# The gate beside the shared expert's weights, a token a partition, and a filter product of three multiplications

## The chip, the cores and the metric

The kernel runs on one core of one Trainium2 chip. The metric is the device time of one execution in microseconds; the time before is the median of three runs. The engines are called PE (TensorE; PEld is its weight load), DVE (VectorE), ACT (ScalarE), POOL (GpSimd) and SP (SyncE, which here only issues transfers).

## The reference

A layer of two halves, in float32, over x of 8 sequences x 512 tokens x 256 channels, each half with a residual and a layer norm after it.

```python
# first half: a gated long convolution
u = x @ W_in + b_in                        # 256 -> 768
x0, x1, v = split(short_conv3(u))          # three taps a channel
v = v * x1
k = (sin(sin(pe @ W1 ...) @ W2 ...) @ W3 + b3) * exp(-t * deltas)   # the filter, 512 x 256
v = irfft(rfft(pad(v), 1024) * conj(rfft(k, 1024)))[:512] + filter_bias
x = layernorm(x + (v * x0) @ W_out + b_out)

# second half: 16 experts, 4 a token, and a shared expert
probs = softmax(x @ gate_w.T)              # 16 logits a token
top_w, top_idx = top_k(probs, 4); top_w = top_w / sum(top_w)
moe = sum over the token's 4 experts of top_w * (silu(x @ w1.T) * (x @ w3.T)) @ w2.T   # hidden 128
shared = (silu(x @ sw1.T) * (x @ sw3.T)) @ sw2.T
x = layernorm(x + moe + shared)
```

The reference computes all experts for every token and weighs them; the kernel sorts the tokens' rows by expert and computes only the chosen four.

## The kernel before

**An order that is planned ahead.** Nothing is scheduled by the framework: `manual_schedule` keeps every engine's instructions in the order in which they are emitted. That order comes from `Plan`, a list scheduler that runs while the kernel is built. Each piece of work is a generator that yields `turn(engine, cost, needs, rings, table, rank)` and then emits its instructions; `Plan.run` keeps a clock for each engine, takes the turn that can start first, breaks ties within 0.05 us by rank, and adds 1.3 us where an activation table must change. Costs are microseconds written by hand into each turn. Buffers are part of it: `ps` are the 8 banks of PSUM, `b2` six buffers of 2 KB a partition, `b4` nine of 4 KB, and a turn waits until one is free. A change of one cost or one need can therefore move everything that comes after it.

**The first half, for each sequence b.** `front` multiplies the input in 128x512 tiles (L418), `convolve_short` evicts each twice (L401, L402) and adds two shifted taps on DVE (L407). The gated v is transposed (L461), and `half_transform` multiplies even and odd tokens with cosines and sines (L484); `joined` adds and subtracts them into `vf`, of real and imaginary part, two halves m of 128 frequencies. `product` multiplies `vf` with the filter's transform. Its first two steps make three operations of 1024 columns for each part (L515 to L517); steps three and four make four operations of 512 columns each (L527 to L530) and complete the second half, c=1. There `g0` holds the filter's first part and `hf` its second part with a sign. `convolved_full` is the way back: for each half i of the channels and each c it takes four matmuls of 256 columns (L560), in the order part 0, part 1 of c=0, then of c=1. `FULL` is 8, so for all eight sequences `product` returns before its last lines, and `convolved` with `inv_sb` is never used. `gated_y`, `normed` and `scaled` finish the half (L598, L666, L625, L642).

**Routing and the shared expert.** `turned` transposes the normed rows x1 into `x1t`, channels on the partitions (L699), and spawns `router` and `shared`. `router` multiplies with the gate: x1t is the stationary side, and 16 columns move (L711), eight matmuls a sequence. DVE copies the logits beside eight columns of -3e38 (L723, L724), takes the top eight, marks the top four (`match_replace`, L741), and ACT takes the exponentials (L735). `shared` multiplies the other way round: sw1 or sw3 is stationary, and 512 tokens move (L797), four matmuls, so that the hidden units are on the partitions as the next product wants them. Then come silu on ACT (L803), one multiply on DVE (L808), sw2 (L818), and the addition to x1 (L842). `route` counts rows and writes each token's four places into `at` (L874); `scatter` sends x1's rows there with 16 indirect transfers on POOL (L996), each 128 rows.

**The experts.** Tokens are taken in four batches: sequences 0 and 1, 2 and 3, 4 and 5, then 6 and 7, the first three with one sort. When a batch's rows are counted, `listed` makes its list of tiles of 128 rows; `fetch` loads four tiles at a time, and `expert_pair` does two: transposes (L1181), w1 and w3 (L1195), silu and multiply (L1206, L1209), a transpose (L1215), w2 (L1227), the weight of the token on ACT or DVE, whichever clock is behind in the plan (L1238, L1240), and indirect transfers home on POOL (L1249). POOL's queue holds the scatters and these transfers in one order. At the end `returned` and `add_up` fetch each token's four results and `finished` norms them.

**The filter.** `filter_transform` runs once, first, and ends with four operations that fill `hf` (L1080) and a copy that fills `g0_sb` (L1088); every product needs them.

The constant and weight loads stand in SP's queue in the order of the code; `w_sb` holds all experts' weights, 17 x 256 columns by three.

Of the kernel before, what the change touches and what calls it, by code (L numbers as in the profile page):

```python
# [20 lines left out]
P = 128  # L21
# [3 lines left out]
NX = NE + 1  # L25
# [3 lines left out]
FULL = 8  # L29
# [174 lines left out]
def layer(  # L204
# [21 lines left out]
    inv: bass.AP,  # L226
# [92 lines left out]
    inv_sb = const.tile([P, 2, CH], F32, name="inv_sb")  # L319
    load(inv_sb, inv.rearrange("(k p) t -> p k t", p=P), "inv")  # L320
# [6 lines left out]
    gate_sb = const.tile([P, KD, NE], F32, name="gate_sb")  # L327
    load(gate_sb, gate, "gate")

    w_sb = const.tile([P, 3, NX * D], F32, name="w_sb")  # L330
    load(w_sb[:, :, NE * D :], experts[NE], "w_shared")
# [171 lines left out]
    def product(b, vf, hf_):  # L503

        needs = [("vf", b, i, m) for i in range(2) for m in range(2)]
        for step in range(4):
            part = step % 2

            op = ALU.add if part else ALU.subtract
            if step < 2:  # L510
                yield turn("DVE", 3 * 1.22, [*needs, "hf"], ["pf"] if step == 0 else ())
                if step == 0:
                    pf, hp = sb("pf", 1, [P, 2, 2, 2, D], f"pf_{b}")
                fa = ring.tile([P, 2, 2, D], F32, tag="fa", name=f"fa_{b}_{part}")
                nc.vector.tensor_mul(fa, vf[:, 1], g0[1 - part])  # L515
                nc.vector.tensor_mul(pf[:, part], vf[:, 0], g0[part])
                nc.vector.tensor_tensor(pf[:, part], pf[:, part], fa, op)  # L517
                if step == 1:
                    plan.done(("vf2", b), late=0.0)
                    if b < FULL:  # L520
                        plan.done(("pf", b, 0))
                        plan.spawn(convolved_full(b, pf, hp), 2 + b * 0.01)
            else:
                yield turn("DVE", 2.1 + 0.69, [("vf2", b)])
                t2 = ring.tile([P, 2, 2, D], F32, tag="fa", name=f"ta_{b}_{part}")
                ta, tb = t2[:, 0], t2[:, 1]
                nc.vector.tensor_tensor(ta, vf[:, 0, :, 0, :], hf[:, part], ALU.mult)  # L527
                nc.vector.tensor_tensor(tb, vf[:, 1, :, 0, :], hf[:, 1 - part], ALU.mult)
                nc.vector.tensor_tensor(ta, ta, tb, op)
                nc.vector.tensor_add(pf[:, part, :, 1, :], pf[:, part, :, 1, :], ta)  # L530
        plan.let(hf_)
        if b < FULL:
            plan.done(("pf", b, 1))
            return

        yield turn("DVE", 2 * 1.22, (), ["b4:pe"])
        pe, he = sb("b4:pe", 0, [P, 2, 2, D], f"pe_{b}")
        nc.vector.tensor_tensor(pe, pf[:, :, 0], pf[:, :, 1], ALU.add)
        plan.done(("pf", b, 0))
        nc.vector.tensor_tensor(pf[:, :, 0], pf[:, :, 0], pf[:, :, 1], ALU.subtract)  # L540
        plan.done(("pf", b, 1))
        plan.spawn(convolved(b, (pe, pf[:, :, 0]), (he, hp)), 2 + b * 0.01)
# [7 lines left out]
    def convolved_full(b, pf, hp):  # L550
        for i in range(KD):
            for c in range(2):
                rings = [*(["ps"] if c == 0 else []), *(["b4:y"] if i == c == 0 else [])]
                yield turn("PE", 8 * PASS[CH], [("pf", b, c), "inv4"], rings)
                if i == c == 0:
                    y, hy = sb("b4:y", 0, [P, KD, T], f"y_{b}")
                if c == 0:
                    y_ps, h = ps([P, T], f"y_ps_{b}_{i}")
                for k in range(4):
                    nc.tensor.matmul(  # L560
                        y_ps[:, c * CH : (c + 1) * CH],
                        lhsT=pf[:, k // 2, k % 2, c, i * P : (i + 1) * P],
                        rhs=inv4_sb[:, k, :],
                        start=k == 0,
                        stop=k == 3,
                    )
            plan.done(("y_ps", b, i))
            plan.spawn(gated_y(b, i, y, y_ps, h), 2 + b * 0.01)
        plan.let(hp)
        plan.spawn(normed(b, y, hy), 2 + b * 0.01)  # L570

    def convolved(b, sums, held):
        for i in range(KD):
            for k in range(2):
                rings = [*(["ps"] if k == 0 else []), *(["b4:y"] if i == k == 0 else [])]
                yield turn("PE", 8 * PASS[P], [("pf", b, k), "inv"], rings)
                if i == k == 0:
                    y, hy = sb("b4:y", 0, [P, KD, T], f"y_{b}")
                if k == 0:
                    y_ps, h = ps([P, T], f"y_ps_{b}_{i}")  # L580
                for c in range(2):
                    for part in range(2):
                        nc.tensor.matmul(
                            y_ps[:, c * CH + k : (c + 1) * CH : 2],
                            lhsT=sums[k][:, part, c, i * P : (i + 1) * P],
                            rhs=inv_sb[:, part, k * P : (k + 1) * P],
                            start=part == 0,
                            stop=part == 1,
                        )
            plan.done(("y_ps", b, i))  # L590
            plan.spawn(gated_y(b, i, y, y_ps, h), 2 + b * 0.01)
        plan.let(*held)
        plan.spawn(normed(b, y, hy), 2 + b * 0.01)
# [97 lines left out]
    def turned(b):  # L691
        x1 = tiles["x1", b][0]
        for k in range(KD):
            yield turn("PE", 4 * PASS[P], [("x1", b)], ["ps", "b4:x1t"] if k == 0 else ["ps"])
            if k == 0:
                x1t, ht = sb("b4:x1t", 0, [P, KD, T], f"x1t_{b}", uses=2)
# [5 lines left out]
        plan.spawn(router(b, x1t, ht), 1)  # L702
        plan.spawn(shared(b, x1t, ht), 1.5)

    def router(b, x1t, ht):

        yield turn("PE", 1.7, [("x1t", b, 0), ("x1t", b, 1), "gate"], ["ps"])
        l_ps, h = ps([P, QT, NE], f"l_ps_{b}")
        for q in range(QT):
            for k in range(KD):  # L710
                nc.tensor.matmul(  # L711
                    l_ps[:, q, :],
                    lhsT=x1t[:, k, q * P : (q + 1) * P],
                    rhs=gate_sb[:, k, :],
                    start=k == 0,
                    stop=k == KD - 1,
                )
        plan.let(ht)
        plan.done(("l", b))
        plan.known["x1t", b] = plan.end  # L720
        yield turn("DVE", 1.3, [("l", b)], ["mask"])
        lg = ring.tile([P, QT, NE + 8], F32, tag="lg", bufs=2, name=f"lg_{b}")
        nc.vector.memset(lg[:, :, NE:], -BIG)  # L723
        nc.vector.tensor_copy(lg[:, :, :NE], l_ps)  # L724
        plan.let(h)
        top = ring.tile([P, QT, 8], F32, tag="top", bufs=2, name=f"top_{b}")
# [55 lines left out]
    def shared(b, x1t, ht):  # L782

        x1, h1 = tiles["x1", b]
        for s in range(2):
            yield turn(
                "PE",
                4 * PASS[T],
                [("x1t", b, 0), ("x1t", b, 1), "w_shared"],
                ["ps", "b2"] if s == 0 else ["ps"],  # L790
            )
            if s == 0:
                act, ha = sb("b2", 0, [P, T], f"acts_{b}")
            h_ps, h = ps([P, T], f"hs_ps_{b}_{s}")
            for k in range(KD):
                at = NE * D + s * HE
                nc.tensor.matmul(  # L797
                    h_ps, lhsT=w_sb[:, k, at : at + HE], rhs=x1t[:, k, :], start=k == 0, stop=k == KD - 1
                )
            plan.done(("hs", b, s))  # L800
            if s == 0:
                yield turn("ACT", 0.61, [("hs", b, 0)], table="silu")
                nc.scalar.activation(act, h_ps, AF.Silu)  # L803
                plan.let(h)
                plan.done(("acts", b))
        plan.let(ht)
        yield turn("DVE", 0.7, [("hs", b, 1), ("acts", b)])
        nc.vector.tensor_mul(act, act, h_ps)  # L808
        plan.let(h)
        plan.done(("actm", b))  # L810
        for q2 in range(QT // 2):
            yield turn("PE", 4 * PASS[D], [("actm", b)], ["ps", "b4:acc"] if q2 == 0 else ["ps"])
# [3 lines left out]
            for j in range(2):  # L816
# [3 lines left out]
                    lhsT=act[:, q * P : (q + 1) * P],  # L820
                    rhs=w_sb[:, 2, NE * D :],
# [208 lines left out]
    def filter_transform():  # L1030
# [45 lines left out]
        yield turn("DVE", 3.2, [("vf", "g", i, m) for i in range(2) for m in range(2)])  # L1076

        for m in range(2):
            for part in range(2):
                nc.vector.scalar_tensor_tensor(  # L1080
                    hf[:, part, m, :],
# [6 lines left out]
        nc.vector.tensor_copy(g0_sb, gf[:, :, :, 0, :])  # L1088
# [4 lines left out]
    hf = const.tile([P, 2, 2, D], F32, name="hf")  # L1093
    g0_sb = const.tile([P, 2, 2, D], F32, name="g0_sb")
    g0 = [g0_sb[:, part, :, None, :].to_broadcast([P, 2, 2, D]) for part in range(2)]
# [253 lines left out]
def shape_constants():  # L1349
# [28 lines left out]
    found = {"places": places, "tri": tri, "seg": np.concatenate(seg), "pos": pos, "decay": decay, "fwd": fwd, "inv": fwd.T / CH, "inv4": inv4, "sign": np.stack([even, -even], 1)}  # L1378
# [40 lines left out]
```

## Time and profile before

| | |
|---|---|
| three runs | 636.99, 639.95 and 643.25 us, median 639.95 |
| the profiled execution | 639.06 us, its span 637.2 us, mean granted clock of PE 0.949 |
| busy in the span | PE 564.1, PEld 423.8, DVE 471.7, ACT 351.9, POOL 320.1 us |
| moved by DMA | 114.33 MB, mean 179 GB/s |
| the chain that ended last | PE 38%, DVE 10%, DMA 4%, ACT 3% of the span, as far as it is followed back |

Busy time is the union of an engine's instructions, so their durations can add up to more. PE's matmuls are pipelined: the mean of one in a group is longer than the distance between two, and the chain, which counts the distance, is the place for prices. Each matmul is two records, a transpose is one. Lines such as L560 are those of the kernel before.

### The profile page before, as it was taken

To read this page: it belongs to the slowest core of one execution; us is meant where nothing else is said; L and a number is where in the kernel's file an instruction comes from. 1 tells how busy PE (TensorE), PEld (TensorE's weight loads), DVE (VectorE), ACT (ScalarE), POOL (GpSimd) and SP (SyncE) were. 2 spreads that over 40 slices of the span, in tenths; PEclk is the share of its full clock that TensorE was granted. 3 is DMA by queue.
4 is the path that set the end of the run, shared out by engine and by line. 5 is a ranking of instruction groups with operands and counts; after the bars stand their busy time and mean duration, and the time that the engine had idled before them with its cause. 6 is when DMAs were issued, how large, how long until landed. Compare 5 with 4: busy or idle time off the path is not lost.

```text
span 637.2 us, 9907 instructions
## 1 busy us (share of the span) xinstructions
PE 564.1 (89%) x2508; PEld 423.8 (67%) x2508; DVE 471.7 (74%) x1267; ACT 351.9 (55%) x737; POOL 320.1 (50%) x580
## 2 busy tenths in 40 slices
PE   5978989849999989899999999999989999889900
PEld 2436566427787756477976866898868888778700
DVE  3997898997986898598479668846633334888786
ACT  2432738404838527653845385275334556899855
POOL 0000018580028887048658841874887876447730
PEclk9997999969999999999999998999989999999955
DMA  7995006223306333335447561532876547999965
GB/s 263 353 333 166 17 34 201 75 102 126 108 29 202 115 133 135 108 111 180 158 150 243 177 214 61 181 132 79 271 227 194 167 140 220 302 356 323 347 230 213
DMA packets 67829, 114.33 MB, mean 179 GB/s; under 512 B 11435, under 2 KB 48569, under 8 KB 67774
## 3 DMA queue, kind: packets, MB, share of 16 engines
q1 hardware_dynamic: 54046, 78.02, 38.6%
q0 software_dynamic: 13728, 35.69, 15.3%
q8 instruction: 22, 0.36, 0.3%
q14 instruction: 33, 0.27, 0.1%
HBM read 61.51 MB, written 56.07 MB: 185 GB/s over the span
## 4 chain that ended last, share of the span: by engine, by line
PE 38%; DVE 10%; DMA 4%; ACT 3%; issue 2%; SPq 1%; POOL 1%; ACTq 0%; DVEq 0%; POOLq 0%
PE h_ps L1195 14%; PE o_ps L1227 7%; PE xr_ps L1181 3%; DMA xr<-xs 3%; PE hs_ps L797 2%; PE y_ps L560 2%; PE u_ps L418 2%; PE h_ps L1215 2%; PE z_ps L666 2%; DVE got L1297 2%; PE v_ps L484 1%; SPq L1127 1%; PE l_ps L711 1%; PE os_ps L818 1%; POOL results L1249 1%
## 5 line engine op out<-in xcount | busy, mean ns | idle before, releaser
L996 POOL DMA_INDIRECT xs<-x,at x128 | 133.7, 1044 | 189.0 <-DVE y L598 92.0
L1249 POOL DMA_INDIRECT results<-o,to x158 | 163.5, 1035 | 102.0 <-ACT o L1238 39.4
L1195 PE MATMUL h_ps<-w_sb,xrt 128*128 x632 | 149.6, 383 | 1.4 <-ACT xrt L1186 1.4
L1195 PEld LDWEIGHTS h_ps<-w_sb,xrt 128*128 128x128 f32 x632 | 118.4, 192 | 18.6 <-ACT xrt L1186 2.6
L418 PE MATMUL u_ps<-xt,w_in_sb 128*128 128x512 f32 x192 | 89.6, 605 | 4.1 <-DMA xt<-in_x_t 4.1
L1227 PE MATMUL o_ps<-w_sb,actt 128*128 x316 | 80.4, 383 | 5.6 <-ACT actt L1220 4.7
L560 PE MATMUL y_ps<-inv_sb,pf 128*128 128x256 f32 x256 | 68.9, 423 | 17.7 <-DVE pf L517 9.4
L401 ACT ACTIVATE u<-u_ps,chan_sb 128x512 f32<-128x512 f32 x48 | 32.9, 686 | 86.0 <-PE u_ps L418 28.2
L560 PEld LDWEIGHTS y_ps<-inv_sb,pf 128*128 128x128 f32 x256 | 51.9, 211 | 32.1 <-DVE pf L530 9.5
L1206 ACT ACTIVATE act<-h_ps 128x256 f32<-128x256 f32 (+1 forms) x80 | 29.9, 380 | 78.0 <-PE h_ps L1195 61.1
L1227 PEld LDWEIGHTS o_ps<-w_sb,actt 128*128 128x128 f32 x316 | 57.7, 190 | 18.3 <-ACT actt L1220 6.0
L418 PEld LDWEIGHTS u_ps<-xt,w_in_sb 128*128 128x128 f32 x192 | 35.8, 194 | 40.0 <-issue 38.2
L1209 DVE TENSOR_TENSOR act<-act,h_ps 128x256 f32<-128x256 f32 (+1 forms) x80 | 32.0, 412 | 34.7 <-ACT act L1206 34.5
L1186 ACT COPY xrt<-xr_ps 128x512 f32<-128x512 f32 (+1 forms) x80 | 44.9, 593 | 9.5 <-PE xr_ps L1181 8.5
L1238 ACT ACTIVATE o<-o_ps,sel 128x256 f32<-128x256 f32 x84 | 34.8, 473 | 23.3 <-PE o_ps L1227 20.5
L1181 PE MATMUL xr_ps<-ident,xr 128*128 128x128 f32 x316 | 45.3, 275 | 1.6 <-ACT xrt L1186 0.7
L1240 DVE TENSOR_TENSOR o<-o_ps,sel 128x512 f32<-128x512 f32 x37 | 25.4, 690 | 26.3 <-PE o_ps L1227 23.2
L1181 PEld LDWEIGHTS xr_ps<-ident,xr 128*128 128x128 f32 x316 | 37.1, 141 | 8.2 <-issue 3.1
L1220 ACT COPY actt<-h_ps 128x256 f32<-128x256 f32 (+1 forms) x80 | 28.7, 375 | 16.0 <-PE h_ps L1215 13.7
L1215 PE MATMUL h_ps<-ident,act 128*128 128x128 f32 x158 | 29.2, 276 | 4.9 <-DVE act L1209 4.9
L797 PE MATMUL hs_ps<-x1t,w_sb 128*128 128x512 f32 x64 | 33.4, 651 | 0.0
L666 PEld LDWEIGHTS z_ps<-w_out_sb,y 128*128 128x128 f32 x128 | 31.0, 327 | 2.3 <-issue 1.2
(164 smaller groups left out, 917.5 us busy)
## 6 DMA issues: line engine op xcount, KB each, us to landing
xr<-xs SPq DMA_DIRECT2D x158, 144.0 KB, 2.8
got<-results SPq DMA_DIRECT2D x32, 512.0 KB, 7.1
xs<-blank SPq DMA_DIRECT2D x62, 144.0 KB, 3.2
w_sb<-in_experts SPq DMA_DIRECT2D x17, 384.0 KB, 7.8
xt<-in_x_t SPq DMA_DIRECT2D x8, 512.0 KB
xn<-in_x SPq DMA_DIRECT2D x8, 512.0 KB, 4.5
kept<-acc SPq DMA_DIRECT2D x6, 512.0 KB, 3.7
sum<-kept SPq DMA_DIRECT2D x6, 512.0 KB, 4.6
```

Of the source, the lines that this page charges most:

```text
L418: nc.tensor.matmul(u_ps, lhsT=w_in_sb[:, k, m * P : (m + 1) * P], rhs=xt[:, k, :], start=k == 0, stop=k == KD - 1)
L560: nc.tensor.matmul(y_ps[:, c * CH : (c + 1) * CH], lhsT=pf[:, k // 2, k % 2, c, i * P : (i + 1) * P], rhs=inv4_sb[:, k, :], start=k == 0, ...
L666: nc.tensor.matmul(z_ps[:, j, :], lhsT=y[:, i, q::QT], rhs=w_out_sb[:, i, :], start=i == 0, stop=i == KD - 1,)
L797: nc.tensor.matmul(h_ps, lhsT=w_sb[:, k, at : at + HE], rhs=x1t[:, k, :], start=k == 0, stop=k == KD - 1)
L996: move = nc.gpsimd.indirect_dma_start(out=xs[i], out_offset=bass.IndirectOffsetOnAxis(ap=at[:, q, k : k + 1], axis=0), in_=x1[:, q, :], in ...
L1181: nc.tensor.transpose(t_ps[:, j, k, :], xr[:, j, k * P : (k + 1) * P], ident)
L1186: nc.scalar.copy(xrt[:, :n], t_ps[:, :n])
L1195: nc.tensor.matmul(h_ps[:, j, :], lhsT=xrt[:, j, k, :], rhs=w_sb[:, k, bass.ds(at[j], D)], start=k == 0, stop=k == KD - 1,)
L1215: nc.tensor.transpose(a_ps[:, j, :], act[:, j, :], ident)
L1227: nc.tensor.matmul(o_ps[:, j, :], lhsT=actt[:, j, :], rhs=w_sb[:, 2, bass.ds(at[j], D)], start=True, stop=True)
L1238: nc.scalar.activation(o[:, j], o_ps[:, j], AF.Copy, scale=sel[:, j0 + j, 0:1])
L1249: move = nc.gpsimd.indirect_dma_start(out=results[i], out_offset=bass.IndirectOffsetOnAxis(ap=to[:, j0 + j : j0 + j + 1], axis=0), in_=o[: ...
```

## The change

Two things are edited, and what was unused is removed.

The gate's 16 columns are loaded behind the shared expert's 256 in `w_sb`. A new `heads` multiplies, for each quarter q of a sequence, x1t as the stationary side with all 272 columns: logits, w1 and w3 come out in one bank of PSUM, a token a partition. `head` copies the logits on ACT, takes silu of 128 columns on ACT and multiplies on DVE, once for each q. The margin of -3e38 is written by POOL when `heads` begins. Since a token is now on a partition, `shared` transposes the four pieces, copies them on ACT, and goes on with sw2 as before.

`product` multiplies complex numbers with three multiplications: of re + im, of im and of re, by the filter's re, re + im and im - re, which are made once in `filter_transform`. Three operations of 1024 columns and twelve of 512 take the place of six and eight, and `vf` is written over. Its costs are new in both turns.

```diff
+    load(w_sb[:, :KD, NX * D :], gate)
+    load(w_sb[:, :, NE * D : NX * D], experts[NE], "w_shared")
...
     def product(b, vf, hf_):
...
+        yield turn("DVE", 4 * 1.22 + 2 * 0.69, [*needs, "hf"], ["pf"])
+        nc.vector.tensor_tensor(fa, re, im, ALU.add)
+        nc.vector.tensor_tensor(pf[:, 0], im, both(g0[:, 1]), ALU.mult)
+        nc.vector.tensor_tensor(pf[:, 1], re, both(g0[:, 2]), ALU.mult)
+        k = im[:, :, 1, :]
+        nc.vector.tensor_tensor(k, fa[:, :, 0, :], g0[:, 0], ALU.mult)
+        nc.vector.tensor_tensor(pf[:, 0, :, 0, :], k, pf[:, 0, :, 0, :], ALU.subtract)
+        nc.vector.tensor_tensor(pf[:, 1, :, 0, :], k, pf[:, 1, :, 0, :], ALU.add)
+        plan.done(("pf", b, 0))
+        plan.spawn(convolved_full(b, pf, hp), 2 + b * 0.01)
+        yield turn("DVE", 9 * 0.69)
+        second = fa[:, :, 1, :]
+        nc.vector.tensor_tensor(second, second, g0[:, 0], ALU.mult)
+        for part, by, of in ((0, 1, im), (1, 2, re)):
+            at = of[:, :, 0, :]
+            nc.vector.tensor_tensor(at, at, hf[:, by], ALU.mult)
+            nc.vector.tensor_tensor(pf[:, part, :, 1, :], pf[:, part, :, 1, :], at, ALU.add)
+        at = fa[:, :, 0, :]
+        nc.vector.tensor_tensor(at, at, hf[:, 0], ALU.mult)
+        nc.vector.tensor_tensor(second, second, at, ALU.add)
+        nc.vector.tensor_tensor(pf[:, 0, :, 1, :], second, pf[:, 0, :, 1, :], ALU.subtract)
+        nc.vector.tensor_tensor(pf[:, 1, :, 1, :], second, pf[:, 1, :, 1, :], ALU.add)
...
+    def heads(b, x1t, ht):
+        lg = ring.tile([P, QT, NE + 8], F32, tag="lg", bufs=2, name=f"lg_{b}")
+        nc.gpsimd.memset(lg[:, :, NE:], -BIG)
         for q in range(QT):
+            yield turn("PE", 1.0, [("x1t", b, 0), ("x1t", b, 1), "w_shared"], ["ps", "b2"] if q == 0 else ["ps"])
+            h_ps, h = ps([P, D + NE], f"hs_ps_{b}_{q}")
             for k in range(KD):
                 nc.tensor.matmul(
+                    h_ps,
                     lhsT=x1t[:, k, q * P : (q + 1) * P],
+                    rhs=w_sb[:, k, NE * D :],
...
+    def head(b, q, lg, act, h_ps, h):
+        yield turn("ACT", 0.25, [("hs", b, q)])
+        nc.scalar.copy(lg[:, q, :NE], h_ps[:, D:])
+        plan.done(("l", b, q))
+        yield turn("ACT", 0.35, (), table="silu", rank=1.5)
+        nc.scalar.activation(act[:, q, :], h_ps[:, :HE], AF.Silu)
+        plan.done(("silus", b, q))
+        yield turn("DVE", 0.25, [("silus", b, q)], rank=1.5)
+        nc.vector.tensor_mul(act[:, q, :], act[:, q, :], h_ps[:, HE:D])
...
     def router(b, lg):
-        nc.vector.memset(lg[:, :, NE:], -BIG)
-        nc.vector.tensor_copy(lg[:, :, :NE], l_ps)
...
     def shared(b, act, ha):
-                    h_ps, lhsT=w_sb[:, k, at : at + HE], rhs=x1t[:, k, :], start=k == 0, stop=k == KD - 1
-                nc.scalar.activation(act, h_ps, AF.Silu)
-        nc.vector.tensor_mul(act, act, h_ps)
+        yield turn("PE", 4 * PASS[P], [("actm", b, q) for q in range(QT)], ["ps"])
+        for q in range(QT):
+            nc.tensor.transpose(a_ps[:, q, :], act[:, q, :], ident)
+        yield turn("ACT", 0.6, [("as_ps", b)])
+        nc.scalar.copy(act, a_ps)
...
+        first = [gf[:, part, :, 0, :] for part in range(2)]
+        nc.vector.tensor_copy(g0[:, 0], first[0])
+        nc.vector.tensor_tensor(g0[:, 1], first[0], first[1], ALU.add)
+        nc.vector.tensor_tensor(g0[:, 2], first[1], first[0], ALU.subtract)
...
+        nc.vector.tensor_tensor(hf[:, 1], hf[:, 0], hf[:, 2], ALU.add)
+        nc.vector.tensor_tensor(hf[:, 2], hf[:, 2], hf[:, 0], ALU.subtract)
```

The four operations that fill `hf` stay, into places 0 and 2. `FULL`, `convolved`, `inv_sb` and `gate_sb` go.

## The prediction

> **What bounds the kernel now.** I read the page's parts 1 and 2 first, then the busy time by stage, then what TensorE (PE) waits for, then the chain for the price of one instruction of each kind, and last the groups by shape.
>
> ```profile
> PE 564.1 (89%) x2508; PEld 423.8 (67%) x2508; DVE 471.7 (74%) x1267; ACT 351.9 (55%) x737; POOL 320.1 (50%) x580
> PE   5978989849999989899999999999989999889900
> DVE  3997898997986898598479668846633334888786
> PEclk9997999969999999999999998999989999999955
> ```
>
> Two engines carry the span, one after the other. By stage (us, then busy us of PE, PEld, DVE, ACT, POOL):
>
> ```profile
> 16.00:300.00 284.00, 260.44 (x1005) 175.41 (x1004) 246.56 (x591) 142.37 (x263) 111.88 (x193) 0.95 0.42 139
> 300.00:447.00 147.00, 144.71 (x694) 115.42 (x693) 103.57 (x312) 83.95 (x180) 89.95 (x163) 0.99 0.48 158
> 447.00:603.00 156.00, 147.71 (x789) 127.76 (x787) 90.35 (x263) 100.59 (x232) 110.00 (x205) 0.99 0.77 253
> ```
>
> Up to 300 us PE and VectorE (DVE) are both nearly full (260 and 247 of 284) and take turns as the limit. From 300 to 603 us PE alone is: 292 of 303. After it 34 us of results coming home and a layer norm, which the change does not touch. What PE waits for in the first 300 us:
>
> ```profile
> PE y_ps L560 <- DVE pf L517: 9.4, 3, 5.4
> PE y_ps L560 <- DVE pf L530: 5.5, 6, 1.6
> ```
>
> So the filter's product on DVE, one of the two edited places, is what PE waits for; the other, the gate with the shared expert, is PE work itself. While PE waits, its clock falls (column after POOL):
>
> ```profile
> 45.00:48.00 3.00, 1.65 (x4) 0.86 (x4) 2.90 (x5) 0.00 (x0) 0.00 (x0) 0.80 0.76 249
> 48.00:51.00 3.00, 1.92 (x5) 1.18 (x4) 2.90 (x5) 0.00 (x0) 0.00 (x0) 0.50 0.92 300
> ```
>
> **PE's part.** The chain prices back-to-back passes (start, us, what):
>
> ```profile
> 317.67 1.69 PE l_ps L711 x16
> 354.58 3.45 PE h_ps L1195 x16
> 390.54 1.72 PE hs_ps L797 x4
> 429.13 0.87 PE x1t_ps L699 x8
> ```
>
> A matmul is two passes in the records, a transpose one. Taken out per sequence: the gate, 16 passes, 1.69 us (0.106 each though only 16 columns move); w1 and w3, 8 passes of 512 columns, 2 x 1.72 = 3.44. Put in: 16 passes of 272 columns. No row has 272; the 256-column row gives 3.45 for 16, the 512-column row 6.88, and 272 is nearest 256: both rows make 0.84 ns a column, so 0.23 each, 3.67 in all (3.45 and 6.88 kept as ends; the upper would lose 2.2 us a sequence). And four transposes back, 4 x 0.109 = 0.44. Net 1.69 + 3.44 - 3.67 - 0.44 = 1.02 us, times 8 = **8.2 us less PE work**. Pricing each program's whole list of PE instructions this way gives 530.1 us before and 521.7 after.
>
> **DVE's part.** Groups by shape (busy, mean ns):
>
> ```profile
> L1209 DVE TENSOR_TENSOR act<-act,h_ps 128x128 f32<-128x128 f32 x2 | 0.6, 283 | 0.6 <-ACT act L1206 0.6
> L515 DVE TENSOR_TENSOR fa<-vf,g_sb 128x1024 f32<-128x1024 f32 x16 | 19.6, 1222 | 0.2
> L527 DVE TENSOR_TENSOR ta<-vf,hf 128x512 f32<-128x512 f32 x16 | 11.0, 688 | 0.3
> L808 DVE TENSOR_TENSOR acts<-acts,hs_ps 128x512 f32<-128x512 f32 x8 | 5.5, 683 | 0.0
> L1206 ACT ACTIVATE act<-h_ps 128x128 f32<-128x128 f32 x2 | 0.6, 302 | 0.0
> L803 ACT ACTIVATE acts<-hs_ps 128x512 f32<-128x512 f32 x8 | 4.8, 597 | 3.3 <-PE hs_ps L797 2.3 <-ACT actt L1220 1.0
> ```
>
> Product before: 6 of 1024 and 8 of 512 columns, 6 x 1.22 + 8 x 0.69 = 12.84 us. After: 3 and 12, 3.66 + 8.28 = 11.94. That is 0.90 less a sequence, 7.2 in all. Its shape changes too. The first half that PE wants (c=0, part 0) was ready after three long operations, 3.66 us; now after three long and two short, 5.04. The last was ready at 12.84, now at 11.94. A PE that stands at the product therefore starts 1.4 us later and ends 0.9 us earlier. The shared multiply becomes four of 128: 4 x 0.283 - 0.683 = +0.45; the copy and the memset of the logits leave DVE (0.214 + 0.085): +0.15 net, 1.2 over 8. The set-up of the filter gains one copy of 512 for one of 1024 (0.69 by L1088, so 0.35 by half) and four operations of 0.69: +2.4, once, ahead of the first product where DVE is full. Sum: -7.2 + 1.2 + 2.4 = -3.6. The planner also moves two more expert outputs from DVE to ACT (35 instead of 37, 0.69 each): about **-5 us on DVE**.
>
> **ScalarE's (ACT) part.** Four copies of 128x16 (no such row; between 0.19 for the accumulator reads of one column at L625 and 0.256 for 128x64 at L735; I take 0.22), four silu of 128 for one of 512 (4 x 0.302 - 0.597 = +0.61), one copy of 512 (0.60, the x1t row of L436): +2.1 us a sequence, 17 in all, and four more L1238 instructions (the two outputs that DVE gives up, 0.473 each), 1.9 once. ACT is busy 55%, and its list holds 47 table loads before and after, so I cost this at nothing in throughput. Its cover is PE's expert tiles between a sequence's heads and its transposes; in sequences 0 to 2 only the four-matmul-pair z (3.4 us) stands there, and ACT needs 4 x (0.22 + 0.30) + 1.28 for the table = 3.4 us for the heads: uncovered, 1 us a sequence is the price.
>
> **POOL and DMA.** Eight memsets of the logits' margin (0.09 each, row L995) join POOL's queue, each behind scatters, and the match (L741) waits for them: a rival below. The unused inverse table, 256 KB, is not loaded (0.9 us at the 284 GB/s of the first 20 us); what follows it in SP's queue lands that much earlier, but w_out is first used at 61 us, with the loads over: nothing. The gate goes into columns of w_sb, first used at 78 us: nothing.
>
> **What of it is on the path.** The planner orders everything anew: batch 0's first expert tile moves from 116 to 135 us of PE work, while product 2 moves from 118 to 96 us of DVE work. So I compared both instruction lists, priced by the rows above, at each product. Before, product b starts at list time plus DVE's idle so far: b=3: 145.6 in the list, 160.0 in the trace, 14.4 idle; b=4: 205.2, 223.9, 18.7; b=5: 250.8, 276.0, 25.2; b=7: 351.4, 396.6, 45.2. PE reaches y of b=7 at 346.8 in its list and 405.7 in the trace, 58.9 idle; the rest is 183.3 of work in 196.3 us (to 602), 13.0 idle.
> After, with DVE's idle kept: product 7 at 337.7 + 45.2 = 382.9, its y 5.0 later at 387.9; with PE's idle kept instead, 325.9 + 58.9 = 384.8. PE's rest is 521.7 - 325.9 = 195.8, plus 13.0: end of PE at 596.7 by DVE, 593.6 by PE, against 602. Gain 5.3 to 8.4; I take the middle, 6.8. The profiled execution took 639.06 (span 637.2 and 1.9 around it), 0.9 below the median of 639.95: 639.06 - 6.8 = **632.3**.
>
> **Rivals.**
> *No change, 638.* The gain is lost where PE waits for DVE and ACT: as_ps waits for silu and multiply of four pieces, 1 us in each of 8 sequences, 8.2 given back but the DVE's 5 partly kept. For: DVE is 87% busy to 300 us, and os_ps already waited 2.3 us for L808. Against: the planner has expert tiles to put there from sequence 3 on. 636 to 642.
> *Clock.* In the trace the stall at product 2 (8.4 us of pieces) brought the clock to 0.50 from 133 to 146 us, and 20 passes of y took 6.16 us where at full clock (237 us) they took 4.58. The changed product leaves PE one gap: c=0 done at 5.55 + 0.86 = 6.6 us after the product's start, c=1 at 10.9: 4.2 us. Sequences 1 and 3, whose y is now listed whole, would pay 1.6 each: +3.2, time 635.5. I count it with no change. [...]
> *More, 626.* The stall of 9 us at product 2 with its slow clock goes, because product 2 is no longer behind batch 0's list of tiles on DVE (22 us earlier there): 6 us more. For: PE's idle at y of sequence 2 is 133.4 - 99.7 = 33.7 before, and by the lists after 96.0 + 11.5 + 5.0 - 87.9 = 24.6. Against: at y of sequence 3 the lists have it at 37.5 again.
> *Slower, 646.* The memset in POOL's queue. For sequence 7 it stands behind nine scatters of sequence 6 and eight results, 17 x 1.27 us (L996's spacing) = 22 us after sequence 6's rows are known; DVE's list has 15 us to the match. For sequence 3: 12 x 1.27 = 15 us against 15.6. POOL ran without a gap from 186 to 253 us before, so it can be late by more; then DVE stands at L741 with the products, the short convolutions and the experts' multiplies behind it, and PE behind those. It decides from about 7 us of POOL lag at each; two waits of 7 us cost 14: 632.3 + 14 = 646. Against: DVE itself ran 45 us behind its list by then, POOL's queue at sequence 7 had gaps.
> That the product is not three multiplications, or the gate not in the same pass, the instruction lists exclude.
>
> **How the numbers follow.** Forecast 632.3 (626 to 636): 0.42. No change with the clock: 0.28. More: 0.14. Slower: 0.16. 1% is 6.4 us, about what a measurement tells here (before: 637 to 643). Faster by over 1%, under 633.5: two thirds of the forecast and all of "more", 0.28 + 0.14 = 0.42, with a little of the rest 0.44. Within 1%: the rest of the forecast and nearly all of "no change", 0.37. Slower, over 646.3: part of the last rival and of what no list shows of the new order, 0.19. The range runs from "more" with some of its 6 us again, 621, to the slower rival, 647.
>
> **What would show it.** Right: the matmuls of hs_ps at 0.23 us a pass in the chain, 128 of them; the product in 12 us; PE's end near 595. Wrong: hs_ps nearer 0.43; as_ps among PE's waits with over 5 us; the match with waits on POOL's memset of over 5 us; PE's idle to y of sequence 7 above 67 us.

## The result, and the profile after

Over 20 runs each, the kernel before took 640.58 us (636.99 to 643.25) and the changed kernel 633.79 us (630.33 to 639.27): 6.8 us less, ratio 0.989, 95% interval 0.988 to 0.991. In a second comparison it was 634.45 against 640.26, ratio 0.992 (0.989 to 0.994). A ratio leaves out runs of more than 1.5% over the fastest of the same kernel, a median counts every run. The profiled execution took 633.87 us, its span 632.1 (before 639.06 and 637.2). In the comparisons behind the experiments 1, 2, 4, 6 and 7, and in the first runs of 3 and 5, ACT and DVE stood for tens of microseconds, from some 155 us on, waiting for a releaser that the trace calls remote (the kernel before took 724 and 713 us there), so of those runs mainly the part before that is read.

Parts 1 and 2 of the page after:

```profile
PE 553.8 (88%) x2476; PEld 426.4 (67%) x2476; DVE 461.9 (73%) x1285; ACT 363.6 (58%) x805; POOL 321.2 (51%) x588
PE   5968999996999998899999969999899999889800
DVE  3998899999968992986997376548243334898786
PEclk9998999999999999799999998989999999999955
```

PE is 10.3 us less busy and DVE 9.8; ACT 11.7 more. The clock's lowest slice before the end was the one from 127 us (6), behind the stall at product 2; that slice is now at 9, and the lowest is the one from 253 us (7), where y of sequence 5 begins. The same three stages (us, then busy us of PE, PEld, DVE, ACT, POOL):

```profile
16.00:300.00 284.00, 261.99 (x1040) 186.65 (x1039) 244.15 (x621) 158.82 (x333) 104.45 (x184) 0.97 0.41 138
300.00:447.00 147.00, 138.97 (x656) 112.48 (x655) 103.26 (x313) 80.47 (x181) 103.66 (x189) 0.98 0.51 170
447.00:603.00 156.00, 144.20 (x766) 123.47 (x764) 87.52 (x263) 104.25 (x243) 109.07 (x203) 0.99 0.77 251
```

Up to 300 us PE now has 22 us idle instead of 24, but from 300 to 603 us 19.8 instead of 10.6 (1.1 of it behind PE's last instruction, which now ends at 601.9). So PE was not faster throughout: part of the work taken from it came back as waiting, late. What it waits for longest, over the whole span (us, times, longest):

```profile
PE y_ps L547 <- DVE pf L526: 10.1, 5, 3.9
PE xr_ps L1150 <- DMA xr<-xs: 8.6, 4, 3.9
```

The filter's product is still the first wait (10.1 us; before it was 9.4 and 5.5 on two lines). The second is new: rows for the experts' tiles, fetched by DMA; from 300 us on it is 6.0 us, against 0.3 before. The groups of the edited head (busy, mean ns):

```profile
L678 PE MATMUL hs_ps<-w_sb,x1t 128*128 128x272 f32 x128 | 30.9, 394 | 1.4 <-ACT x1t L431 1.4
L697 ACT ACTIVATE acts<-hs_ps 128x128 f32<-128x128 f32 x32 | 8.5, 287 | 0.0
L694 ACT COPY lg<-hs_ps 128x16 f32<-128x16 f32 x32 | 5.6, 179 | 12.3 <-PE hs_ps L678 12.1
```

### The profile page after: what moved, and what is told of

The parts are those of the page before. It is cut to its first block, busy times and chain, and to the rows that moved or that the text cites. A ratio compares the mean times of both kernels' runs of the same rounds, so it can differ in the third digit from the quotient of the medians.

```text
span 632.1 us, 9976 instructions
## 1 busy us (share of the span) xinstructions
PE 553.8 (88%) x2476; PEld 426.4 (67%) x2476; DVE 461.9 (73%) x1285; ACT 363.6 (58%) x805; POOL 321.2 (51%) x588
## 4 chain that ended last, share of the span: by engine, by line
PE 36%; DMA 9%; DVE 7%; ACT 4%; POOL 2%; issue 2%; SPq 1%; ACTq 0%; POOLq 0%; DVEq 0%
PE h_ps L1164 13%; PE o_ps L1196 6%; PE y_ps L547 4%; DMA xr<-xs 3%; PE xr_ps L1150 3%; DMA got<-results 3%; DVE got L1266 2%; POOL results L1218 2%; PE z_ps L630 2%; PE hs_ps L678 2%; PE u_ps L413 2%; PE h_ps L1184 2%; DMA results<-o,to 2%; SPq L1096 1%; PE os_ps L782 1%
## 5 line engine op out<-in xcount | busy, mean ns | idle before, releaser
L960 POOL DMA_INDIRECT xs<-x,at x128 | 135.3, 1057 | 223.8 <-DVE x L402 100.4
L1164 PE MATMUL h_ps<-w_sb,xrt 128*128 x632 | 148.8, 382 | 0.1
L1164 PEld LDWEIGHTS h_ps<-w_sb,xrt 128*128 128x128 f32 x632 | 118.7, 192 | 17.5 <-issue 2.4
L547 PE MATMUL y_ps<-inv_sb,pf 128*128 128x256 f32 x256 | 66.8, 419 | 15.8 <-DVE pf L526 10.1
L1150 PE MATMUL xr_ps<-ident,xr 128*128 128x128 f32 x316 | 47.3, 281 | 9.2 <-DMA xr<-xs 8.6
L1155 ACT COPY xrt<-xr_ps 128x512 f32<-128x512 f32 (+1 forms) x80 | 44.9, 591 | 12.8 <-PE xr_ps L1150 12.0
L1207 ACT ACTIVATE o<-o_ps,sel 128x256 f32<-128x256 f32 x88 | 36.6, 474 | 23.1 <-PE o_ps L1196 15.9
L1113 DVE TENSOR_TENSOR part<-xr,one 128x128 f32<-128x128 f32 (+3 forms) x41 | 11.8, 287 | 43.4 <-DMA xr<-xs 43.3
L1209 DVE TENSOR_TENSOR o<-o_ps,sel 128x512 f32<-128x512 f32 x35 | 24.0, 689 | 15.5 <-PE o_ps L1196 14.4
L678 PE MATMUL hs_ps<-w_sb,x1t 128*128 128x272 f32 x128 | 30.9, 394 | 1.4 <-ACT x1t L431 1.4
```

The costliest lines, as they stand in the source:

```text
L547: nc.tensor.matmul(y_ps[:, c * CH : (c + 1) * CH], lhsT=pf[:, k // 2, k % 2, c, i * P : (i + 1) * P], rhs=inv4_sb[:, k, :], start=k == 0, ...
L678: nc.tensor.matmul(h_ps, lhsT=x1t[:, k, q * P : (q + 1) * P], rhs=w_sb[:, k, NE * D :], start=k == 0, stop=k == KD - 1,)
L960: move = nc.gpsimd.indirect_dma_start(out=xs[i], out_offset=bass.IndirectOffsetOnAxis(ap=at[:, q, k : k + 1], axis=0), in_=x1[:, q, :], in ...
L1150: nc.tensor.transpose(t_ps[:, j, k, :], xr[:, j, k * P : (k + 1) * P], ident)
L1155: nc.scalar.copy(xrt[:, :n], t_ps[:, :n])
L1164: nc.tensor.matmul(h_ps[:, j, :], lhsT=xrt[:, j, k, :], rhs=w_sb[:, k, bass.ds(at[j], D)], start=k == 0, stop=k == KD - 1,)
```

## The experiments

Three theories. "Work": PE has 8 us less to do, and PE sets the time. "Product": VectorE's path through the filter's product to the second half of the output sets it. "Order": the planner's other order of the work made the difference. The first eight runs are told in short, the last four, on one chip without those waits, decide.

**1. The gate edit alone**, twice: the changed kernel with the old product and its set-up, planned anew.

```diff
-        yield turn("DVE", 4 * 1.22 + 2 * 0.69, [*needs, "hf"], ["pf"])
-        nc.vector.tensor_tensor(fa, re, im, ALU.add)
...
+                yield turn("DVE", 3 * 1.22, [*needs, "hf"], ["pf"] if step == 0 else ())
+                nc.vector.tensor_mul(fa, vf[:, 1], g0[1 - part])
```

> The gate beside w1 and w3 as in the change, the filter's product as before; the planner makes a new order. Theory 'work': the change gains what it takes from TensorE, 8.2 us by the chain's prices, so this alone gives nearly all of it: 632 to 635 against 640.6 before. Theory 'order': the gain comes from the new order of the planner, and any other edit gives another order, so the time is anywhere from 634 to 644. Theory 'product': the gain is VectorE's, and this gives 639 to 642.

> The gate beside w1 and w3, the product as before, in a new order, once more on another chip: the first look fell on a chip on which the kernel before took 724 us, with stalls of several us on ScalarE whose releaser is outside the kernel. Work: 632 to 636 where the kernel before takes 640; product: 639 to 642; order: anything from 634 to 644.

Measured: ratio to before 0.997 (0.993 to 1.001) and 0.988 (0.983 to 0.993); the two hardly agree, so no size is taken. The early part agrees better: product 3 starts at 148.8 and 146.7 us, where before has 159.9 and the changed kernel 143.5.

**2. The product edit alone**: the kernel before with the new product and set-up, planned anew (the diff of the change without its gate part).

> The product of three multiplications as in the change, gate and shared expert as before; the planner makes a new order. Work: VectorE has 7.2 - 2.4 = 4.8 us less, which counts only where the product is what TensorE waits for (two sequences before): 638 to 641. Product: 633 to 636. Order: anywhere from 634 to 644.

Measured: 0.987 (0.982 to 0.993). Product 3 starts at 159.7 us, as before, because the set-up costs 3.0 us first. Inconclusive as to the size.

**3. The old product in the changed kernel's place**: the same order of all other instructions on every engine, the two turns with the same costs, the old operations and the old set-up in them. It was run twice; only the second time undisturbed.

```diff
+        for part, op in ((0, ALU.subtract), (1, ALU.add)):
+            nc.vector.tensor_mul(fa, vf[:, 1], both[1 - part])
+            nc.vector.tensor_mul(pf[:, part], vf[:, 0], both[part])
+            nc.vector.tensor_tensor(pf[:, part], pf[:, part], fa, op)
...
+            nc.vector.tensor_tensor(ta, vf[:, 0, :, 0, :], hf[:, part], ALU.mult)
+            nc.vector.tensor_tensor(tb, vf[:, 1, :, 0, :], hf[:, 1 - part], ALU.mult)
+            nc.vector.tensor_tensor(ta, ta, tb, op)
+            nc.vector.tensor_add(pf[:, part, :, 1, :], pf[:, part, :, 1, :], ta)
```

> The changed kernel with the old product and the old set-up emitted in the turns of the new one, at the new one's planned costs, so that every other instruction on every engine stands where it stands in the changed kernel. Work: VectorE has 4.8 us more; the first half of the product is there 2.3 us later (7.3 instead of 5.0 for both parts), the last 0.9 later: 634 to 638 against 633.8. Product: 638 to 641. Order: 633 to 635, as the order is the same.

First time: 0.994 (0.988 to 1.000).

> The changed kernel in its own order of work, with the old filter product and its set-up: per sequence 0.9 us of VectorE work more, at the set-up about 2.4 us less, 4.8 us more in all. 'Product' (VectorE's chain to the second half of the filter's output sets the time at most sequences): 4 to 8 us over the changed kernel. 'Work on TensorE': 0 to 3 us over it, since TensorE's list is the same.

Second time: 637.92 us, ratio 0.996 (0.994 to 0.998), beside the changed kernel again:

> The changed kernel itself, as the reference for the other three kernels of this comparison. Both theories expect its ratio to the kernel before to be 0.985 to 0.992, as it was measured first.

634.45 us. So the old product costs 3.5 us by the medians, midway between the two ranges that were expected (0 to 3 and 4 to 8). The intervals of the two ratios just touch; by the single runs, the 95% interval of the difference is about 1 to 5.5 us, so the product is worth something, and the size fits either range. But the two traces have one order of work and can be laid side by side. Starts of the products 0 to 7 with the old product, less those with the new: -2.7, -1.8, -0.3, +3.2, +3.6, +3.4, +3.8, +3.8 us; PE's last instruction +4.8. The new set-up costs 2.7 us, three sequences win 5.9 us against that, and from product 3 on nothing more is won until the end. The sizes are rough: the changed kernel's own two profiles have product 3 at 143.5 and 145.5 us. How one sequence wins it is seen in PE's timeline (start, us, what, and the idle time before it). Sequences 2 and 3 with the new product:

```profile
114.32 1.89 PE L547 MATMUL y_ps<-inv_sb,pf 128*128 128x256 f32 x8
117.79 5.45 PE L547 MATMUL y_ps<-inv_sb,pf 128*128 128x256 f32 x24 [1.58 <-DVE pf L526]
150.45 1.97 PE L547 MATMUL y_ps<-inv_sb,pf 128*128 128x256 f32 x8 [0.91 <-DVE pf L512]
156.33 7.13 PE L547 MATMUL y_ps<-inv_sb,pf 128*128 128x256 f32 x24 [3.91 <-DVE pf L526]
```

Sequence 2 with the old product:

```profile
113.79 1.89 PE L538 MATMUL y_ps<-inv_sb,pf 128*128 128x256 f32 x8
116.88 1.13 PE L538 MATMUL y_ps<-inv_sb,pf 128*128 128x256 f32 x4 [1.20 <-DVE pf L518]
119.66 7.52 PE L538 MATMUL y_ps<-inv_sb,pf 128*128 128x256 f32 x20 [1.65 <-DVE pf L518]
```

Both products start at 107 us. The old one hands over its second half in two portions, PE stops twice (1.20 and 1.65 us), and then 20 passes take 7.52 us where 24 take 5.45. That is the granted clock, the column after POOL in the busy time by stretch. The new product, from 118 to 124 us:

```profile
118.00:124.00 6.00, 6.00 (x29) 5.22 (x29) 5.89 (x9) 3.96 (x6) 5.12 (x9) 1.00 0.27 103
```

The old one in the same stretch:

```profile
118.00:124.00 6.00, 4.35 (x11) 3.53 (x11) 5.82 (x10) 2.77 (x5) 5.12 (x9) 0.57 0.29 110
```

From the product's start to the end of y it is 20.5 us with the old and 16.3 with the new product, of which DVE's own saving is 1.5 (12.8 against 11.3 us, below); the rest, 2.7, is the clock and the second stop. In sequence 3 both fall back in clock (0.80 from 154 to 160 us with the new product, 0.50 from 160 to 166 with the old) and the difference is 2.0. The old product stood in this place in three more traces, which are undisturbed up to here. In the first runs of experiments 1 and 3 the gaps are again 1.2 and 1.65 us, and the clock is halved for 6.8 us; in the second run of experiment 1 they are 0.63 and 1.65 us, and 20 passes take 4.58 us at full clock. In experiment 6 a single gap of 2.56 us, at sequence 1 and again at 2, was followed by a halved clock for 3.4 us, as the single gap of 3.91 us above was by the 0.80 of sequence 3. So the fall is not tied to two stops. It came after stops of 1.2 and 1.65 us all three times, after those of about 0.6 and 1.65 in one of five places of these traces; from what length of stop on it comes, no run shows.

**4. The new product in the place of the old, in the order of the kernel before**: its four turns and their costs kept, three, three, five and four of the new operations in them.

```diff
         yield turn("DVE", 3 * 1.22, [*needs, "hf"], ["pf"])
+        nc.vector.tensor_tensor(fa, re, im, ALU.add)
+        nc.vector.tensor_tensor(pf[:, 0], im, both(g0[:, 1]), ALU.mult)
+        nc.vector.tensor_tensor(pf[:, 1], re, both(g0[:, 2]), ALU.mult)
         yield turn("DVE", 3 * 1.22, [*needs, "hf"], ())
...
```

> The kernel before with the new product in the turns of the old one at the old planned costs: every other instruction stands where it stands before; the unused inverse table is not loaded. Work: VectorE has 4.8 us less and the product ends 0.9 us earlier, its first part 1.4 later: 637 to 641. Product: 633 to 636. Order: 639 to 642, as the order is the same.

Measured: 0.979 (0.973 to 0.984), but the waits from outside differ between the kernels of that comparison, so the size is not read. Early part, against the profile before: product 0 starts 2.8 us later, product 2 1.4 later, product 3 0.2 later, and sequence 2's places (`at`) come 1.4 us earlier, at 184.0. That is about 1 us a sequence.

**5. The gate's columns as matmuls of their own**, in the changed kernel and its order, run twice.

```diff
                 nc.tensor.matmul(
-                    h_ps,
+                    h_ps[:, :D],
                     lhsT=x1t[:, k, q * P : (q + 1) * P],
-                    rhs=w_sb[:, k, NE * D :],
+                    rhs=w_sb[:, k, NE * D : NX * D],
...
+                nc.tensor.matmul(
+                    h_ps[:, D:],
+                    lhsT=x1t[:, k, q * P : (q + 1) * P],
+                    rhs=w_sb[:, k, NX * D :],
```

> The changed kernel with the gate's 16 columns as matmuls of their own behind the 256 of w1 and w3, in the same bank and the same turn; every other instruction on every engine stands where it stands. TensorE gets 16 passes of 0.106 more a sequence and 16 passes of 256 instead of 272 columns (0.014 less each): 1.47 us a sequence, 11.8 in all. Theory 'work' (TensorE's work sets the time one to one in the later part and about half before): 7 to 12 us more than the changed kernel. Theory 'order' (what counts is which instruction stands where, not a few us of TensorE): 0 to 3 more.

First time its six runs took 704 to 724 us among the waits from outside, too far apart for a ratio; up to 178 us, after some 4.4 us of added work, its trace runs 1.9 us behind the changed kernel's first profile and not at all behind its second.

> The changed kernel, with the 16 gate columns of each pass multiplied by matmuls of their own, so that each sequence's head takes 16 passes of 256 columns and 16 of 16 columns, all else in the changed kernel's order. From the rows of the kernel before, where those 16 columns cost 0.106 us a pass as matmuls of their own, TensorE gets about 1.5 us of work more a sequence by the list, 12 us in all. 'Work' (TensorE's work counts where TensorE sets the time, half or more of the span): 6 to 12 us over the changed kernel. 'Order' (the change gained by another order of the work, and what TensorE does in the heads is covered): 0 to 3 us over it.

Second time: 636.81 us, ratio 0.994 (0.992 to 0.996): 2.4 us over the changed kernel, and under 5 even between the far ends of the two intervals. "Work" (6 to 12) fell; whether it is 2.4 us or nothing the runs do not tell apart (by the single runs, the 95% interval is -0.8 to 3.7). The dose was given; the groups:

```profile
L678 PE MATMUL hs_ps<-w_sb,x1t 128*128 128x256 f32 x128 | 34.9, 395 | 1.4 <-ACT x1t L431 1.4
L686 PE MATMUL hs_ps<-w_sb,x1t 128*128 128x16 f32 x128 | 16.5, 242 | 0.0
```

The heads of sequence 2 take 5.15 us (124.31 to 129.46) instead of 3.67, 1.48 more, 11.8 in all; PE is busy 565.7 us instead of 555.3. But y 7 begins at 384.3 us instead of 383.9, seven doses later, and PE ends at 604.8 instead of 603.8. Four of the added microseconds went into idle time between 210 and 300 us (7.5 to 3.4), and most of the rest into the wait for rows, here the line of PE's waits:

```profile
PE xr_ps L1158 <- DMA xr<-xs: 3.4, 4, 2.0
```

It is 8.6 us in the changed kernel. The chain that ended last shows, in the changed kernel's second run, why PE's work does not matter there (start, us, what):

```profile
368.50 0.68 ACT x L397
...
374.46 1.28 POOL xs L960
376.04 3.42 DMA xs<-x,at
...
380.02 2.29 DMA xr<-xs
...
382.35 0.44 PE xr_ps L1150 x2
...
384.07 2.88 PE y_ps L547 x8
```

POOL's queue (rows home, then rows out) ends, the last rows go to memory and come back by DMA, and only then does PE transpose them and go on to y 7. The step from ACT to POOL is no wait for ACT: POOL pauses as long between any two transfers, as its timeline shows.

```profile
369.25 0.98 POOL L1218 DMA_INDIRECT results<-o,to  x1 [0.24 <-ACT x L397]
370.54 1.06 POOL L1218 DMA_INDIRECT results<-o,to  x1 [0.24 <-issue]
```

From 291.2 to 378.0 us it makes 64 transfers, 1.35 us apart, with no pause over 0.26 us: it is POOL's queue that sets the time here. With the added work the same 64 run from 291.8 to 378.3. In the kernel before they ran from 279.0 to 373.9 with pauses of up to 5.9 us, so there the queue was not full. PE comes to the rows about 4 us later with the added work and waits some 3 us less; first without it, then with it:

```profile
381.75 0.44 PE L1150 MATMUL xr_ps<-ident,xr 128*128 128x128 f32 x2 [3.92 <-DMA xr<-xs]
382.76 0.89 PE L1158 MATMUL xr_ps<-ident,xr 128*128 128x128 f32 x4 [0.52 <-DMA xr<-xs]
```

**6. More work on DVE**: one 1024-column addition more in each product of the changed kernel, written over by the next operation.

```diff
         nc.vector.tensor_tensor(fa, re, im, ALU.add)
+        nc.vector.tensor_tensor(pf[:, 0], re, im, ALU.add)
```

> The changed kernel with one more operation of 1024 columns (its result is written over by the next) at the start of each product; all else stands where it stands. VectorE gets 8 x 1.22 = 9.8 us more, and each product ends 1.2 later. Work: VectorE limits in the first sequences and TensorE later: 2 to 6 us more than the changed kernel. 'Product' (VectorE sets the time up to sequence 7): 8 to 10 more. 'Order': 0 to 1.

Measured: 1.005 (1.000 to 1.010) against before, among the waits from outside. Up to product 3 the doses, three of 1.22 us, put the trace 6.0 us behind the changed kernel's first profile (149.55 against 143.54) and 4.1 behind its second: 3.7 us of work cost at least that much, as in experiment 3.

**7. Another order alone**: the kernel before, the first two turns of its product priced 0.5 us cheaper for the planner, the same instructions in another order.

```diff
-                yield turn("DVE", 3 * 1.22, [*needs, "hf"], ["pf"] if step == 0 else ())
+                yield turn("DVE", 3 * 1.22 - 0.5, [*needs, "hf"], ["pf"] if step == 0 else ())
```

> The kernel before with 0.5 us less in the plan's cost of the product's first two turns: the same instructions in another order of the planner. Work: the same work, so within 3 us of the kernel before. Order: a new order is a new draw, 5 us or more to either side.

Measured: 1.004 (1.000 to 1.009), no gain, in the disturbed comparison; its sequence 2 had its places 4.8 us earlier than before (180.6 against 185.4). In that comparison another order was no gain by itself.

**8. The first frequency half first**: the way back takes c=0 of both channel halves, then c=1 of both, so that 16 passes instead of 8 can run before the product's second half is needed; the planner orders the rest.

```diff
+        held = {}
+        for c in range(2):
+            for i in range(KD):
-        for i in range(KD):
-            for c in range(2):
...
-                    y_ps, h = ps([P, T], f"y_ps_{b}_{i}")
+                    held[i] = ps([P, T], f"y_ps_{b}_{i}")
+                y_ps, h = held[i]
```

> The changed kernel, with the output matmuls of the filter taken in another order: the first frequency half of both channel halves, then the second frequency half of both, so that twice as many passes (16, not 8) can run before the second half of the product is needed. The planner is left to order the rest by it. 'Product' (TensorE's waits for the second half, 10.1 us in the changed kernel's profile, are what is left of it): 3 to 8 us under the changed kernel, with those waits near 2 us. 'Work on TensorE' or 'order': the waits move elsewhere, and the time is within 3 us of the changed kernel's, or over it where the new order puts other work late.

Measured: 630.8 us, ratio 0.984 (0.980 to 0.988), beside 0.992 (0.989 to 0.994) of the changed kernel: the fastest kernel here, 3.7 us under it by the medians of all runs and 5.1 by the ratios. With six runs, from 626.8 to 636.5 us, the size is rough. Its y of sequence 2 in PE's timeline:

```profile
112.80 3.62 PE L549 MATMUL y_ps<-inv_sb,pf 128*128 128x256 f32 x16
116.77 3.72 PE L549 MATMUL y_ps<-inv_sb,pf 128*128 128x256 f32 x16 [0.35 <-DVE pf L526]
```

And what PE waits for, over the span:

```profile
PE y_ps L549 <- DVE pf L526: 5.6, 4, 2.2
PE xr_ps L1153 <- DMA xr<-xs: 3.0, 4, 2.0
```

The stop is 0.35 us instead of 1.58, and over the eight sequences y's matmuls are busy 61.2 us instead of 67.9, for the same passes. The wait for the product is halved, though not down to 2 us. How that becomes 3.7 us at the end is not settled: the new order also starts product 3 at 164.0 us instead of 145.5, by the transposes of sequence 7 (415 us) the two kernels are level, and the gain appears after them, with more of the experts' work already done.

## Why the prediction was right

The forecast of 632.3 was 1.5 us under the median, and the gain of 6.8 us came out as forecast (5.8 in the second comparison). That it came out so close is luck: its two parts did not weigh what the sum gave them, and errors on both sides cancelled.

- *PE's part.* The heads cost what was worked out: 16 passes in 3.67 us. That the time follows PE's list, with the idle time kept, is the step that failed: experiment 5 gives back 11.8 us of such work for 2.4 us. By that share, 0.2 (0.3 at the far end of its interval), the 8.2 us are worth about 1.7 us (an estimate, as if the share held for the smaller dose). "From 300 to 603 us PE alone is" the limit was read from the kernel before; in the changed kernel POOL's queue sets the time from 291 to 378 us.
- *DVE's part.* The product's saving was mis-sized: 0.90 us a sequence forecast, 1.5 measured (start to end, where nothing else stands between, 12.83 before, 11.33 after). The sum took the means of single operations, 1.22 and 0.69; operations that neither read nor overwrite what the other uses start 1.14 and 0.60 apart, the others 1.26 and 0.72, and the new product has more of the first kind. The set-up was right (2.4 forecast; product 0 starts 2.2 to 3.0 later). The durations of DVE's instructions add up to 5.8 us less, near the 5 forecast, but with the overlap DVE is 9.8 us less busy. By experiment 3 this part is worth 3.5 us, won in the first three sequences and in part through PE's clock.
- *What is left.* 3.5 and 1.7 make 5.2 of the 5.8 us of that comparison. Gate and order together, by experiment 3 against before, are 2.3 us; what of that is the order alone was not separated, and the 1.7 is an estimate, so how the gain divides is shown only for the product.
- *The end.* That PE would end "at 596.7 by DVE, 593.6 by PE, against 602" was wrong on both sides: PE's last instruction ended at 607.33 before and at 601.86 after. The idle time behind y 7, set at 13.0 us, was 18.3 before and 24.5 after. Of the 6.2 us more, 1.9 is a wait for rows; the rest lies inside PE's busy time, with the clock halved for 9.4 us there instead of 3.4. Against that, product 7 started at 372.5, not 382.9, and y 7 at 381.5, not 384.8 to 387.9: DVE had been idle 34.8 us by then (372.5 less 337.7 of the list), not the 45.2 that were kept. The errors cancel in the difference: 5.5 us between these two executions.
- *ACT.* The durations of its instructions add up to 17.5 us more, near the 19 forecast; they overlap, so it is 11.7 us busier. PE's waits for ACT add up to 10.5 us instead of 9.9, so little of it shows there; no run takes this work away again.
- *The rivals.* "No change" has its place refuted: as_ps stands in none of the changed kernel's waits of PE. "Slower" too: DVE shows no wait for POOL, each memset (0.15 us, not 0.09) began at least 3.1 us before its match. "More" was right that the stall at product 2 goes (gaps of 5.42 and 1.53 us before, 1.56 after) and right in its doubt: at sequence 3 there is one of 3.9. *Clock* was right in its mechanism: the first half's y at 4.97 us after the product's start (its half forecast at 5.04), the second at 10.84 (10.9), and after a gap of 3.91 us 24 passes in 7.13 instead of 5.45 us, 1.7 (1.6), but of the two sequences that it named at 3 only; at 1, PE was still busy with other work, stopped for 1.30 us and stayed at full clock. It missed that the old product paid as much or more.

## What to carry to other kernels

Where two engines take turns as the limit, look for the places where a queue or a transfer ends last, and add the work back to learn its worth: here PE's work was worth about 0.2 us a microsecond. POOL, busy 51% of the span, was the limit from 291 to 378 us, with no pause over 0.26 us: look for an engine's pauses in a stretch, and not at its share. Count in how many portions a result reaches TensorE: at sequence 2 the second stop and the clock that fell with it cost 2.7 us, the saved operations 1.5. Price a run of operations by the distance between their starts: the 512-column operations here are 0.69 us long, and the independent ones overlap, 0.60 us from start to start.

## What the runs showed that was not expected

- Gaps of 1.20 and 1.65 us with four passes between them were followed by a lower clock in all three traces that have them (0.57 from 118 to 124 us in the second run of experiment 3), while after one gap of 1.58 us it stayed at 1.00. After one gap of 2.56 us it was halved for 3.4 us, twice.
- DVE's operations of 512 columns are 0.69 us long, but start 0.60 us apart where neither operation reads or overwrites what the other uses, 0.72 where one does; those of 1024 columns 1.14 and 1.26.
- In the changed kernel POOL's queue runs 87 us without a pause over 0.26 us, where it had pauses of up to 5.9 us before.
- In the runs with waits from outside, ACT and DVE stood 50 to 90 us in all for what the trace calls remote, single waits up to 13.6 us, and the kernel before took 713 to 724 instead of 640 us. What releases them was not found.
